# A quantized macaron block with an S4 convolution: byte planes stored by halves, norms with a power on GpSimd, statistics and scales dealt anew

## The chip, the cores and the metric

The kernel runs on one core of a Trainium2 chip. The metric is device time in microseconds (us) of one execution, lower is better; a time that is given for a kernel is the median of several executions. PE is TensorE (PEld its weight loads), DVE is VectorE, ACT is ScalarE, POOL is GpSimd, SP is SyncE, which computes nothing here and issues most of the DMAs.

## What is computed

The input `u` has 2 x 1024 rows of 1024 values, so 2048 tokens. Three residual steps follow each other:

```python
x = x + 0.5 * ffn(layernorm(x))   # 4-bit weights, three matrices
x = x + s4(layernorm(x))          # long convolution over the 1024 values of a row, plus D * row
x = x + 0.5 * ffn(layernorm(x))   # the same weights again

def ffn(x):      # hidden size 1024, inner size 2752
    h = silu(x @ Wg) * (x @ Wu)
    return h @ Wd
# W[k, n] = scales[k // 128, n] * (w4[k, n] - (z4[k // 128, n] + 1))
```

A 32-bit word of a weight matrix holds eight 4-bit numbers, of eight successive rows of one column. Zero points are packed alike, along columns. The layer norm is `(x - mean) / sqrt(var + 1e-5)`.

## The kernel before

The 2048 tokens are four blocks of 512. A *job* is one feed-forward step of one block; eight jobs run in a fixed order (`JOBS`, L782). A job has a gate/up part of 64 *steps* and a down part of 44. In gate/up, the inner size is cut into eight *waves* (0 to 4 with three pairs of column tiles, 5 to 7 with two), and each wave runs over the eight groups of 128 hidden rows, one group a step. A step of waves 0 to 4 is 12 matmuls of 128x128 by 512 (`gate_up`, L826): six column tiles ("units"), each with the high and the low half of the normed input (`xTh`, `xTl`). After each group the sum in PSUM is multiplied by a ratio of scales (`rat`; `scaled`, by ACT at L786 or DVE at L790), so that the weights themselves are plain signed bytes. The down part (L911) works alike with `ratd`.

The bytes are made once, in job 0, and kept in DRAM (`w_q`, `wd_q`), from which every step of every job loads its tile (`load_bytes`, L747 and L754, four steps ahead) and casts it to fp32 (`make_weights`, three steps ahead, by POOL at L763, in job 0 by ACT at L761 for steps that are 1, 2 or 5 modulo 8). Making the bytes of a wave goes like this: `fetch` loads the packed words, `fetch_zeros` loads the table of zero points from DRAM, spread over partitions; `split` (L617 to L632) takes the even and the odd nibbles apart on DVE, adds the zero points and flips signs, in six pieces; `dequantize` (L657) copies each of the eight byte planes (one row out of eight) into a tile `q` on POOL; `keep_bytes` (L667) stores the plane to `w_q` with one DMA from SP. The table of zero points comes from `zero_points_in_pieces` (L381): eight small DVE operations `zi` (L359), one large one `ztab` (L368), and a store to `z_dram` (L388). Wave 0 has its own route (`first_split`, L583), which also puts the bytes of its first group straight into `first_tile`, 16 partitions a plane. The down matrix goes through `fetch_down`, `split_down`, `dequantize_down` (L670 to L698) in six blocks.

What is done when is written by hand. `first_weights` (L700), and `fast` (L1559) for the norms and scales, hang small pieces onto steps: a piece at step 3 is written before that step's matmuls, at 3.5 in their middle. A compiler pass then orders each engine's instructions by its own estimate. Where `in_order_of_writing` (L143) wraps a piece, its instructions keep the written order on the named engines. In job 0 the byte loads keep it on SP for the first 52 steps (L796). Each engine, and SP's queue, works through its instructions in order, so an instruction that waits holds up those behind it.

The work ahead of job 0 is `start` (L1814), pinned in written order on ACT, DVE, SP and PE: loads, `first_split`, the statistics (`first_moments`, two tiles by ACT, two by DVE), the first scales (`scales_in_pieces`, L415), the inverse deviation (`guess` makes a start value by integer arithmetic, `deviations` improves it in three rounds, L219), the normed rows (`first_rows`), and their turn by PE (`first_turn`; ACT copies the high half, DVE subtracts for the low half; chunk 5 goes through POOL). `keep_warm` only keeps PE working.

Of the kernel before, what the change touches and what calls it, by code (L numbers as in the profile page):

```python
# [12 lines left out]
I32 = mybir.dt.int32  # L13
# [44 lines left out]
def macaron_s4_kernel(  # L58
# [43 lines left out]
    qpool = ctx.enter_context(tc.tile_pool(name="q", bufs=4))  # L102
# [79 lines left out]
    def moments_by_tile(b, k, halves=False):  # L182
# [11 lines left out]
        yield from guess_in_pieces(b, k, mv)  # L194

    def guess(b, k, mv):
        for _ in guess_in_pieces(b, k, mv):
            pass

    def guess_in_pieces(b, k, mv):  # L200
        name = f"{b}_{k}"
        ve = small.tile([P, NT], F32, tag="ve", name=f"ve_{name}")
        nc.vector.tensor_scalar(ve, mv[:, :, 1], EPS, None, ALU.add)
        yield
        r = small.tile([P, NT], F32, tag="r", name=f"r_{name}")
        half = small.tile([P, NT], I32, tag="half", name=f"half_{name}")
        nc.vector.tensor_scalar(half, ve.bitcast(I32), 1, None, ALU.logical_shift_right)
        yield
        nc.vector.tensor_scalar(
            r.bitcast(I32), half, -1.0, float(0x5F3759DF), ALU.mult, ALU.add  # L210
        )
        ln[b] = (mv, ve, r)

    def deviations(b, k, factor=1.0):
        for _ in deviations_in_pieces(b, k, factor):
            pass
        return ln[b, 0, "r"]

    def deviations_in_pieces(b, k, factor=1.0, single=False):  # L219
# [3 lines left out]
        for three in (3.0, 12.0, 768.0):  # L223
            nc.vector.tensor_tensor(e, r, r, ALU.mult)
            if single:
                yield
            nc.vector.tensor_tensor(e, e, ve, ALU.mult)
            if single:
                yield
            nc.vector.scalar_tensor_tensor(r, e, three, r, ALU.subtract, ALU.mult)  # L230
            yield
        nc.vector.tensor_scalar(r, r, -factor / 8192, None, ALU.mult)
# [182 lines left out]
    def scales_in_pieces(k0, k1, rows, copy):  # L415
# [14 lines left out]
        copy(flat(s), ps[:, : (u1 - u0) * GK])  # L430
        yield
        inv = t2(f"inv_{k0}")[:, : (u1 - u0) * GK]
        yield from inverse_in_pieces(inv, flat(s), k0)
        yield
        own = rat[:, u0:u1]
        inv = inv.rearrange("p (u g) -> p u g", g=GK)
        nc.vector.tensor_tensor(own[:, :, : GK - 1], s[:, :, : GK - 1], inv[:, :, 1:], ALU.mult)
        nc.vector.tensor_scalar(
# [144 lines left out]
    def first_split(zq):  # L583
# [8 lines left out]
        for part in (even, raw):  # L592
            both = part.bitcast(U16)
            nc.vector.tensor_tensor(both, both, z.bitcast(U16), ALU.add)
        nc.vector.tensor_scalar(both, both, 0x8080, None, ALU.bitwise_xor)

        def rest():
            upper = even.bitcast(U16).rearrange("p (n k) -> p n k", k=2)[:, :, 1]
            nc.vector.tensor_scalar(upper, upper, 0x8080, None, ALU.bitwise_xor)

        def dequantize(j):
            q = t2(f"q_0_{j}").bitcast(I8)[:, :n]
            view = lambda a, dt: a.bitcast(dt).rearrange("p (n k) -> p k n", k=4)[:, j // 2, :]
            if j in (0, 2):
                nc.scalar.activation(q, view(even, U8), AF.Identity, bias=minus_128)
            else:
                nc.gpsimd.tensor_copy(q, view(raw if j % 2 else even, I8))
            nc.sync.dma_start(first_tile[j:P:8], q[: P // 8])
            bytes_of[j] = q

        def keep(j, queue):
            queue.dma_start(w_q[0].rearrange("(r j) n -> j r n", j=8)[j], bytes_of.pop(j))

        bytes_of = {}
        return rest, dequantize, keep
# [40 lines left out]

    def dequantize(w, j):  # L657

        q = qpool.tile([P, width_of(w)], I8, tag="q", name=f"q_{w}_{j}")
        nc.gpsimd.tensor_copy(q, packed[w][j % 2][:, j // 2, :])  # L660
        ready[w, j] = q
        if j == 7:
            packed.pop(w)

    ready = {}

    def keep_bytes(w, j):  # L667
# [1287 lines left out]
```

## Time and profile before

| what | us |
|---|---|
| median of 3 runs | 2049.24 (2048.68 to 2050.22) |
| the profiled execution, its own time | 2049.47 |
| span of its profile | 2047.6 |
| PE, DVE, ACT, POOL busy | 2005.8, 1644.0, 1414.3, 1352.4 |
| first gate/up matmul starts | 21.30 |
| wave 0 / waves 1 to 7 of job 0 end | 56.6 / 201.7 |
| job 0 ends | 291.2 |

The profile is one execution. A row of a stage table has busy times in that stretch. A row of a group has its place in the code, the engine, output and inputs, the count, then the busy time in us and the mean of one in ns, and the idle time before it. A row of the chain shows what the end of the program hung on, followed back; a DMA there is named by what it writes and reads. Names are those of the program with numbers left out: `zi` and `ztab` are the unpacked zero points and their table, `z` the table as read back, `wq` the bytes in DRAM, `b` a tile of bytes, `w_up` the cast weights, `q` a byte plane, `pg` and `po` sums in PSUM.

### The profile page before, as it was taken

The numbers are of one execution on the slowest core, as the hardware profiler recorded it, in microseconds if no ns is written. First come the engines' busy times: TensorE is split into PE (matmuls) and PEld (weight loads), VectorE is DVE, ScalarE is ACT, GpSimd is POOL, SyncE is SP. The second block draws the span as 40 slices with busy tenths as digits, with TensorE's granted clock in tenths as the row PEclk, the third lists the DMA queues.
The fourth block names the chain that finished last, engine by engine and source line by source line (L and its number), as shares of the span: only waits on it lengthen the run. The fifth ranks groups of instructions, "written<-read, shape, count | busy, mean of one in ns | idle before, by whom it ended". The sixth has DMA issues, their size and how long they took to land.

```text
span 2047.6 us, 29913 instructions
## 1 busy us (share of the span) xinstructions
PE 2005.8 (98%) x9198; PEld 1371.3 (67%) x9198; DVE 1644.0 (80%) x2826; ACT 1414.3 (69%) x2217; POOL 1352.4 (66%) x1739
## 2 busy tenths in 40 slices
PE   5999999999999999999999999999999999999998
PEld 3555675567866778665876568667686676866576
DVE  8877978867888787887878777887878978777776
ACT  5788787747676476777777777664776637767775
POOL 4867768757875478755967568763696646965542
PEclk9999999999999999999999999999999999999999
DMA  4335323233624327411462126333163331661113
GB/s 136 114 98 151 114 81 88 56 84 91 174 78 87 88 50 184 150 32 35 117 181 88 32 48 158 97 83 91 38 160 103 72 94 43 155 193 38 34 36 102
DMA packets 347270, 197.14 MB, mean 96 GB/s; under 512 B 168069, under 2 KB 325038, under 8 KB 347102
## 3 DMA queue, kind: packets, MB, share of 16 engines
q1 hardware_dynamic: 345414, 192.55, 35.1%
q10 hardware_dynamic: 1592, 2.41, 0.3%
q8 instruction: 75, 1.23, 0.3%
q14 instruction: 93, 0.76, 0.1%
q0 software_dynamic: 96, 0.20, 0.0%
HBM read 127.52 MB, written 48.57 MB: 86 GB/s over the span
## 4 chain that ended last, share of the span: by engine, by line
PE 92%; DVE 3%; DMA 2%; ACT 1%; issue 1%; POOL 1%; SPq 0%; ACTq 0%; DVEq 0%; POOLq 0%
PE pg L826 57%; PE po L911 30%; PE pc L1279 3%; PE pb L1279 1%; ACT pg L786 1%; DMA b<-wq 1%; DVE pg L790 1%; POOL q L660 0%; DVE hf L861 0%; DMA x<-in_L_attn_u_dram 0%; ACT g L858 0%; POOL w_up L763 0%; DMA z<-z_dram 0%; DVE po L790 0%; PE pt L247 0%
## 5 line engine op out<-in xcount | busy, mean ns | idle before, releaser
L786 ACT ACTIVATE pg<-pg,rat 128x512 f32<-128x512 f32 x1280 | 807.2, 660 | 386.6 <-PE pg L826 382.5
L790 DVE TENSOR_TENSOR pg<-pg,rat 128x512 f32<-128x512 f32 x1128 | 748.5, 692 | 137.3 <-PE pg L826 129.4
L826 PE MATMUL pg<-xTh,w_up 128*128 128x512 f32 x2752 | 848.2, 436 | 3.7 <-ACT pg L786 1.8
L826 PE MATMUL pg<-xTl,w_up 128*128 128x512 f16 x2752 | 710.7, 382 | 10.7 <-ACT pg L786 5.5
L826 PEld LDWEIGHTS pg<-xTh,w_up 128*128 128x128 f32 x2752 | 518.9, 189 | 172.0 <-ACT pg L786 9.0
L763 POOL CAST w_up<-b 128x768 fp32r<-128x768 int8 (+2 forms) x490 | 375.7, 772 | 381.9 <-PE pg L826 261.9
L786 ACT ACTIVATE po<-po,ratd 128x512 f32<-128x512 f32 x669 | 437.8, 662 | 144.5 <-PE po L911 144.0
L911 PE MATMUL po<-hl,w_down 128*128 128x512 f32 x1344 | 526.8, 394 | 1.9 <-DVE po L790 1.8
L911 PE MATMUL po<-hh,w_down 128*128 128x512 f32 x1344 | 521.1, 390 | 0.0
L790 DVE TENSOR_TENSOR po<-po,ratd 128x512 f32<-128x512 f32 x611 | 423.9, 696 | 112.3 <-PE po L911 111.9
L826 PEld LDWEIGHTS <-w_up 128*128 128x128 bf16 x2752 | 227.1, 98 | 346.8 <-issue 163.0
L763 POOL CAST w_down<-bd 128x512 fp32r<-128x512 int8 x352 | 218.6, 624 | 145.1 <-PE po L911 75.7
L911 PEld LDWEIGHTS po<-hl,w_down 128*128 128x128 f32 x1344 | 251.9, 188 | 65.9 <-DVE po L790 6.6
L911 PEld LDWEIGHTS po<-hh,w_down 128*128 128x128 f32 x1344 | 252.4, 188 | 50.5
L865 POOL TENSOR_TENSOR hl<-hf,hh 128x512 fp32r<-128x512 f32 x168 | 218.0, 1298 | 6.6
L863 POOL CAST hh<-hf 128x512 fp32r<-128x512 f32 x168 | 108.7, 647 | 85.7 <-DVE hf L861 58.8
L861 DVE SCALAR_TENSOR_TENSOR hf<-pg,rat,g 128x512 f32<-128x512 f32 x168 | 121.0, 745 | 50.3 <-ACT g L858 43.2
L858 ACT ACTIVATE g<-pg,rat 128x512 f32<-128x512 f32 x168 | 110.1, 688 | 33.5 <-PE pg L826 17.6
L964 POOL TENSOR_TENSOR x<-x,yr 128x512 f32<-128x512 f32 x52 | 66.8, 1285 | 0.0
L299 POOL TENSOR_TENSOR lo<-x,hi 128x512 f16<-128x512 f32 x48 | 62.2, 1297 | 0.0
L189 DVE BATCH_NORM_STATS2 stats<-x 128x6 f32<-128x512 f32 x88 | 59.9, 681 | 0.0
L297 POOL TENSOR_TENSOR mid<-hi,top 128x512 bf16<-128x512 f32 x48 | 56.1, 1168 | 0.0
(215 smaller groups left out, 1075.9 us busy)
## 6 DMA issues: line engine op xcount, KB each, us to landing
b<-wq SPq DMA_DIRECT2D x319, 96.0 KB
bd<-wdq SPq DMA_DIRECT2D x336, 64.0 KB
x<-in_L_attn_u_dram SPq DMA_DIRECT2D x30, 512.0 KB
yz<-y SPq DMA_DIRECT2D x56, 256.0 KB
yr<-yz SPq DMA_DIRECT2D x56, 256.0 KB
b<-wq SPq DMA_DIRECT2D x128, 64.0 KB
sz<-xn SPq DMA_DIRECT2D x16, 512.0 KB
st<-sz SPq DMA_DIRECT2D x64, 128.0 KB
```

What stands on the lines that cost most here:

```text
L299: nc.gpsimd.tensor_tensor(lo[:, own], n[:, own], hi[:, own].bitcast(F32), ALU.subtract)
L763: nc.gpsimd.tensor_copy(t, b)
L786: nc.scalar.activation(dst, src, AF.Copy, scale=sc)
L790: nc.vector.tensor_tensor(dst, src, sc.to_broadcast(list(dst.shape)), ALU.mult)
L826: product = lambda: nc.tensor.matmul(p, weights, (lo, hi)[k][:, g, :], start=(g == 0 and not done), stop=(g == GK - 1 and done), skip_grou ...
L858: nc.scalar.activation(g, pg, AF.Silu, scale=rat[:, 2 * f, GK - 1 :])
L861: nc.vector.scalar_tensor_tensor(hf, pu, last, g, ALU.mult, ALU.mult)
L863: nc.gpsimd.tensor_copy(hi, hf)
L865: nc.gpsimd.tensor_tensor(lo, hf, hi.bitcast(F32), ALU.subtract)
L911: nc.tensor.matmul(ps[c], w[:, bass.ts(c, P)], part, start=(f == 0 and k == 0), stop=(f == NF - 1), skip_group_check=True,)
L964: nc.gpsimd.tensor_tensor(part, part, rows_back.pop((a, t)), ALU.add)
L1279: nc.tensor.matmul(dst, lhsT, rhs, start=start, stop=stop, skip_group_check=True)
```

## The change

The change has six parts.

1. **Stores.** The eight planes of a wave go into one wide tile (from the pool of `y`, which has one buffer), and are stored by two DMAs, one for the four even planes and one for the four odd. In the down matrix, and in wave 0, two planes share a store. The wave's copies and stores get other steps; wave 1's last two split pieces come half a step later.
2. **Load order.** Byte loads keep the written order on SP only in the first 8 steps.
3. **Wave 0 and the start.** All even planes are made by ACT (from unsigned bytes, with a bias of -128), all odd ones by POOL. Wave 1's words are fetched by SP. ACT takes the statistics of one tile, DVE of three. POOL's written order is pinned too. Four of the eight `zi` come ahead of the first turn. Chunk 3 is turned through POOL like chunk 5. In step 0 the high half is multiplied first.
4. **Norms.** `guess` scales the variance and takes its power -0.5 on POOL; `deviations` is one cubic step, of four small DVE operations. The factor `LIFT` moves into `guess`.
5. **Scales.** The copy from PSUM goes to ACT, and the guarded value and the ratios to POOL; DVE keeps the reciprocal.
6. **Down.** Copies come a step later from the third block on, and the third block's split moves to steps 1 to 4.

```diff
-    qpool = ctx.enter_context(tc.tile_pool(name="q", bufs=4))
+    qpool = ctx.enter_context(tc.tile_pool(name="q", bufs=3))
...
-        nc.vector.tensor_scalar(ve, mv[:, :, 1], EPS, None, ALU.add)
...
+        nc.vector.tensor_scalar(ve, mv[:, :, 1], EPS, (8 / (3 * factor)) ** 2, ALU.add, ALU.mult)
         r = small.tile([P, NT], F32, tag="r", name=f"r_{name}")
...
+        nc.gpsimd.tensor_tensor(r, ve, minus_half, ALU.pow)
...
-        for three in (3.0, 12.0, 768.0):
-            nc.vector.tensor_tensor(e, r, r, ALU.mult)
...
+        nc.vector.tensor_tensor(e, r, r, ALU.mult)
+        yield
+        nc.vector.tensor_tensor(e, e, ve, ALU.mult)
+        yield
+        nc.vector.scalar_tensor_tensor(f, e, -10.0 / 3, e, ALU.add, ALU.mult)
+        yield
+        nc.vector.scalar_tensor_tensor(r, f, 5.0, r, ALU.add, ALU.mult)
...
-        copy(flat(s), ps[:, : (u1 - u0) * GK])
...
+        nc.scalar.copy(flat(s), ps[:, : (u1 - u0) * GK])
+        yield
+        safe = t2(f"safe_{k0}")[:, : (u1 - u0) * GK]
+        nc.gpsimd.tensor_tensor(safe, flat(s), flat(s), ALU.mult)
+        nc.gpsimd.tensor_scalar(safe, safe, 2.0**-60, None, ALU.is_lt)
+        nc.gpsimd.tensor_tensor(safe, safe, flat(s), ALU.add)
+        yield
+        nc.vector.reciprocal(safe, safe)
...
+        nc.gpsimd.tensor_tensor(own[:, :, : GK - 1], s[:, :, : GK - 1], safe[:, :, 1:], ALU.mult)
+        nc.gpsimd.tensor_scalar(
...
-        for part in (even, raw):
+        for part in (raw, even):
             both = part.bitcast(U16)
             nc.vector.tensor_tensor(both, both, z.bitcast(U16), ALU.add)
...
-            if j in (0, 2):
+            if j % 2:
+                nc.gpsimd.tensor_copy(q, view(raw, I8))
+            else:
                 nc.scalar.activation(q, view(even, U8), AF.Identity, bias=minus_128)
...
-        q = qpool.tile([P, width_of(w)], I8, tag="q", name=f"q_{w}_{j}")
-        nc.gpsimd.tensor_copy(q, packed[w][j % 2][:, j // 2, :])
...
+        if w not in unpacked:
+            q = ypool.tile([P, 4 * TB], F32, tag="y", name=f"q_{w}").bitcast(I8)[:, : 8 * n]
+            unpacked[w] = q.rearrange("p (two a n) -> p two a n", two=2, a=4)
+        nc.gpsimd.tensor_copy(unpacked[w][:, j % 2, j // 2, :], packed[w][j % 2][:, j // 2, :])
...
+    def keep_bytes(w, odd):
+        rows = w_q[w].rearrange("(r a two) n -> two r a n", a=4, two=2)[odd]
+        nc.sync.dma_start(rows, unpacked[w][:, odd])
...
-            steps = (0.5, 1, 2, 2.5, 2.5, 3) if w == 1 else range(6)
+            steps = (0.5, 1, 2, 2.5, 3, 3.5) if w == 1 else range(6)
...
-            copies = {1: (3,) * 8, 2: (3, 3, 4, 4, 6, 6, 7, 7)}
...
+            copies = {1: (3.5,) * 8, 2: (3, 3, 4, 4, 6, 6, 7, 7)}.get(w, (3, 3, 4, 5, 6, 6, 7, 8))
...
+            for odd, o in enumerate({1: (3.5, 3.5), 2: (5.5, 7.5)}.get(w, (6.5, 9.5))):
+                at(up, s0 + o, lambda w=w, odd=odd: keep_bytes(w, odd))
...
+            return dn, n - 14 if n >= 24 else n - 12 if n > 15 else (0, 0, 1, 2)[n - 12]
...
+                if n == 16:
+                    steps = [(dn, d) for d in (1, 1.5, 2, 2.5, 3, 4)]
...
-            if j == 0 and s < 52:
+            if j == 0 and s < 8:
                 w = in_order_of_writing(next_weights, ET.SP)
...
+            if j == s == 0:
+                turns = [(1 - k, pos, done) for k, pos, done in turns]
...
-        if c != 5:
+        if c not in (3, 5):
...
         dequantize_first, keep_first = first_split(zq)
         for j in (1, 3):
             dequantize_first(j)
+        fetch(1)
         for j in (5, 7):
             dequantize_first(j)
+        first_scales = scales_in_pieces(0, 3, srow)
+        mv, scratch = first_moments()
         next(first_scales)
         for j in (0, 2):
+            dequantize_first(j)
+        next(first_scales)
+        guess(0, 1, mv, LIFT)
+        for _ in first_scales:
+            pass
+        keep_first(1, 0, nc.gpsimd)
+        dequantize_first(4)
+        keep_first(0, 0, nc.sync)
+        dequantize_first(6)
+        keep_first(1, 1, nc.gpsimd)
+        keep_first(0, 1, nc.scalar)
...
         points = zero_points_in_pieces(0, zeros)
-        for _ in range(9):
+        for _ in range(4):
             next(points)
+        first_turn(0)
+        for _ in range(5):
+            next(points)
...
-    points, zeros_down = in_order_of_writing(start, *STARTING, ET.PE)
+    points, zeros_down = in_order_of_writing(start, *STARTING, ET.PE, ET.Pool)
```

## The prediction

> **What bounds the kernel now.** I first cut the span into stages, because an average hides them. Each row gives the stretch, its length, then busy time and instruction count of PE, PEld, DVE, ACT and POOL, then the granted clock and the DMA share.
>
> ```profile
> 0.00:21.30 21.30, 5.11 (x29) 4.60 (x30) 14.51 (x46) 11.16 (x19) 8.07 (x17) 1.00 0.54 186
> 21.30:56.60 35.30, 27.99 (x131) 17.18 (x131) 28.99 (x55) 22.75 (x38) 17.12 (x21) 0.95 0.38 113
> 56.60:104.50 47.90, 45.07 (x200) 26.26 (x199) 41.76 (x66) 37.46 (x61) 41.65 (x44) 1.00 0.38 110
> ...
> 149.60:201.70 52.10, 49.61 (x211) 27.22 (x209) 39.77 (x64) 42.98 (x71) 40.64 (x55) 1.00 0.56 154
> ...
> 291.20:1000.00 708.80, 706.93 (x3281) 480.05 (x3281) 575.06 (x1017) 487.55 (x766) 478.80 (x632) 1.00 0.35 91
> ```
>
> From 291 us on PE idles 1.87 us in 709. There the kernel runs at PE's pace: in job 3, 287 gate/up matmuls take 64.54 us, 0.225 each. What can be won lies in the first 291 us. The first matmul starts at 21.30. Wave 0, the next 35.3 us, holds 8 x 12 = 96 gate/up matmuls, or 21.6 us of work, so 13.7 us are lost (PE's busy time hides half of this: a delayed matmul counts as busy). By the same count waves 1 to 7 (592 matmuls, 133.2 us of work) take 145.1 us from 56.6 to 201.7, so about 12 us are lost, in pieces. Of the last 47.6 us PE is idle 8.5, and the change does not touch the end.
>
> Next I read the chain that ended last, in order of time (start, length, what), for wave 0:
>
> ```profile
> 21.64 2.81 DVE zi L359 x8
> 24.47 1.06 DVE ztab L368
> 25.55 1.82 DMA z_dram<-ztab
> 28.07 4.29 DMA z<-z_dram
> 33.06 4.33 DMA b<-wq
> 37.55 0.92 POOL w_up L763
> 38.47 0.77 POOL q L660
> ...
> 46.62 0.86 POOL q L660
> 47.49 1.62 DMA wq<-q
> 49.75 2.04 DMA b<-wq
> 53.31 3.18 PE pg L826 x7
> ```
>
> This is the making of wave 1's bytes: zero points on DVE, out to DRAM, back spread over partitions, the split, eight byte planes copied by POOL from 38.4 to 47.5, the last plane stored, read back, cast. PE stands still from about 49.9 to 53.3 for it; ACT has the cast of the second of these tiles (L761) at the head of its queue, and the rescales of wave 0 stand behind. Wave 0's end is thus set by this chain, not by the first matmul.
>
> Third, the waits of SP's queue, of POOL and of ACT in the first part (total us, times, longest):
>
> ```profile
> SPq L668 <- POOL q L660: 50.5, 30, 8.8
> ```
> ```profile
> POOL q L660 <- DMA wq<-q: 6.0, 3, 3.3
> ```
> ```profile
> ACT w_up L761 <- DMA b<-wq: 11.0, 5, 3.1
> ```
>
> SP waits 50.5 us in 30 plane stores for POOL's copies, with the byte loads pinned behind them; POOL waits 6.0 us for a free `q` buffer; ACT waits 11.0 us for bytes while rescales stand behind it.
>
> **The change, part by part.**
>
> *The start.* Today DVE has the last statistics at 15.13, because ACT takes two tiles at 2.43 us each, and starts only at 10.22, behind its issue of wave 1's raw words at 9.84. That issue goes to SP, and x's second tile landed at 8.52, so ACT's one tile can be done at 8.55 + 2.43 = 11.0. DVE takes three tiles: split done near 8.8, then 1.28 + 0.21 each, the third having landed at 10.7, so 13.3. The norm loses the shift and magic-number steps: today 3 + 10 small ops at 0.2 us, 15.33 to 17.9; after it 1 + 4 on DVE and one power on POOL. The power has no row. The nearest is POOL's two-input op on few elements:
>
> ```profile
> L1139 POOL TENSOR_TENSOR s_work<-s_work 128x8 f32<-128x8 f32 x28 | 5.1, 204 | 0.6
> L1170 POOL TENSOR_TENSOR s_work<-s_work 128x64 f32<-128x64 f32 x2 | 0.6, 324 | 0.0
> ```
>
> At 0.2 us plus two hand-overs of about 0.1, deviations and bias are ready near 15.1 instead of 18.1. A rule speaks against this: the Trainium skill, GPSIMD Engine Reference, section 2.1 Instruction dispatch, says that the first call of a freshly loaded POOL kernel costs about 6 us without a row of its own. In this trace POOL's first two-input op (L1806, 40.87) took 1.30 us like its later ones (1.29), and its first copy 0.82, so no load shows. By the row the rows start at 15.1; by the rule near 21. I take 0.2 us, as power is an operator of an instruction already in use; no gain is possible below 0.2, and 6 stays as the upper end.
>
> ACT now makes all four even planes (4 x 0.875 from about 11.2, to 14.7) and issues one store, so it is free near 15.2: level with DVE. The last tile piece leaves SP at about 15.4 and lands 1.5 to 2 us later; POOL's cast takes 0.98. The first matmul can start near 18.1, 3.2 earlier.
>
> *DVE between 18 and 26.* Four of the eight zero-point ops (0.36 each) come ahead of the first `xTl`, in time in which DVE would wait for ACT's `xTh` (17.5); that puts `xTl` at 18.0 to 18.7. The four others and the table (1.06) follow, to 21.2, against 25.5 today: 4.3 us earlier, 3 from the start and 1.3 from the scale ops (0.20 + 0.71 + 0.20 + 0.17) that go to POOL. The high half first in step 0 lets PE begin before `xTl` is there, worth 0.6 us, but not on the longer chain, so counted at nothing.
>
> *Wave 1's bytes.* Store and loads of the table follow 4.3 us earlier. The eight copies (6.6 us) and one chunk's turn (2.2 us) remain; chunk 3's turn now falls on POOL too, 2.2 us, at a time in which it waits for bytes (25.2 to 34.4, idle 9.3). If that cover went, 2.2 us would come onto the chain. The odd planes are then stored in one 384-KB piece after the eighth copy. The Trainium skill, DMA: Bandwidth & Descriptors, section Bandwidth, says to batch towards 1 MiB, and with its fixed cost of about 2 us a transfer (section Anatomy of one DMA) six transfers fewer would look like 12 us. The chain shows only the last of eight stores on the path, 1.62 us. The merged one has 24 more packets on each of 16 engines, and a 768-byte packet takes 0.035 us in this trace, so it costs 0.85 more: by the rule a gain, by the row a loss. I take the loss. Sum to wave 1: -4.3 + 0.85 = **-3.4**; bounds -5 (the copies no longer interleaved with the turn) and -1.5 (POOL's scale ops of step 5.5 slip between the copies).
>
> *Waves 2 to 7.* Two stores a wave in place of eight, and byte loads free to go ahead of them after step 8. ACT blocked on bytes is what stops PE in steps 22 and 23 (2.3 us) and 47 (1.5), where the loads at 97.3 and 161.4 left SP right after stores that had waited for late copies. Smaller losses of the kind make 0.6. POOL's wait for `q` buffers within a wave goes as well, but with one wide tile the next wave's first copy waits for both stores: copies of wave 2 end at 70.9 and those of wave 3 start at 71.9, so POOL would stand some 1.5 us there; the casts run about 4 us ahead of PE and hide it. Of 4.4 us I take **-2**; bounds 0 and -4.4. The loads that are freed can also be placed worse; that is a rival below.
>
> *Down, start.* Three pieces of the third block's split leave step 0, where DVE ran splits between rescales and PE showed gaps of 0.88 and 1.20 us at 206.4 and 208.1. Less the usual 0.23 each that is 1.6; **-1**, bounds 0 and -1.6. Copies come a step later; blocks are needed 6 or more steps on, so this costs nothing.
>
> *Norms later on.* Eight small DVE ops fewer in each of 11 norms lie beside PE's work. Only two last ops (L232, 1.23 us where the median is 0.17) held PE, by 0.61 and 0.60 at 884 and 1119: 0.8 in all. That length may belong to the place and not to the op: **-0.4**, bounds -0.8 and +0.4.
>
> *Scales on POOL.* Three groups of about 96 columns, two ops of 0.39, one of about 0.3, then 0.37 and 0.24: 1.7 us each, where POOL is busy 41.65 of 47.9 us. DVE sheds about 1 us each. **+0.6**, bounds -0.5 and +2.
>
> Sum: -3.4 - 2 - 1 - 0.4 + 0.6 = **-6.2**. The profiled execution took 2049.47 us (span 2047.6 and 1.87 around it), 0.23 above the median of 2049.24. So 2043.3 for such an execution, **2043.0** as a median.
>
> **The rivals.**
>
> *All late-byte stalls vanish* (-4.4 in waves 2 to 7, -1.6, -0.8, and -4.4 to wave 1, nothing lost on POOL): -11.2, 2038. For it: SP's 50.5 us behind copies; against it: POOL itself is nearly full from 60 to 80 us, and DVE's slow splits there stay.
>
> *The start gains, wave 1 does not follow.* POOL's scale ops come between its copies (+1.7) and chunk 3's turn loses its cover (+2.2): -6.2 + 3.9 is -2.3, 2047. For it: POOL works without a break from 37.5 to 47.5; against it: it idles 9.3 us just before.
>
> *The power costs 6 us.* The start loses 5.8: 2049.
>
> *Slower: a half-wave store blocks SP.* A store now waits for the fourth copy of its kind, and with load order free a load can stand behind it. Then ACT and PE stop as at 49.8: 3.3 us and 0.5 for twelve matmuls at the lowered clock of 0.83. This would be at the boundaries of waves 2 to 7. From two such blocks on, 7.6 us against a gain of 6.2, the change loses; with the 2 us of waves 2 to 7 lost as well and three blocks it is 2049.2 - 4.2 + 11.4, 2056. Against it: copies of a wave end some 8 us ahead of the next wave's in most waves (wave 3's at 84.1, wave 4's start at 94.5).
>
> **How the numbers follow.** The forecast has a chance of 0.52, all stalls gone 0.20, wave 1 not following 0.14, the costly power 0.04, the blocking store 0.10. A measurement of this kernel can tell about 0.2%, 4.1 us, from no change: faster means below 2045.1, slower above 2053.3. Faster: 0.44 of the forecast's 0.52, the 0.20, and 0.03 of the third, 0.67. Slower: 0.09. Same: 0.24. The forecast's own range is 2039.5 to 2046. The range for 8 in 10 is 2037 to 2048.5: it leaves out the blocking store, half the costly power and the best of the second case, about 0.18.
>
> **What would show it.** In the changed profile: first gate/up matmul near 18; the zero-point table done near 21; PE's stop for wave 1's bytes ending near 50 instead of 53.3; ACT's wait for bytes well under 11 us; the power near 0.2 us; no gaps at the start of down; from 285 us on the same stretches, shifted. The forecast is wrong if the table is early but the POOL copies are not, if new waits of POOL for the wide tile appear, or if SP's loads stand behind half-wave stores.

## The result, and the profile after

The changed kernel takes 2046.55 us (2043.29 to 2047.56, median of 16 runs) where the kernel before took 2049.86 on the same chip (median of 16). The ratio is 0.9981, with a 95% interval from 0.9974 to 0.9989: 0.1 to 0.3% faster. The interval lies below 1, but the gain is less than the 0.2%, or 4.1 us, that the prediction took as the least that can be told. The forecast was 2043.0. The profiled execution of the changed kernel took 2046.72 us, with a span of 2044.9, 2.7 less than before.

The stages of the changed kernel: the start, steps 0 to 8 (wave 0, and the step in which the stop for wave 1's bytes ends), steps 9 to 23 (waves 1 and 2), steps 24 to 62, and a part of the rest. Columns as before: busy time and count of PE, PEld, DVE, ACT, POOL, then the granted clock, the DMA share, GB/s.

```profile
0.00:19.75 19.75, 6.78 (x33) 6.06 (x33) 14.56 (x45) 11.39 (x18) 9.42 (x22) 1.00 0.57 196
19.75:54.07 34.32, 31.29 (x142) 19.18 (x143) 27.81 (x42) 23.98 (x41) 23.62 (x30) 0.95 0.40 119
54.07:101.60 47.53, 43.85 (x188) 25.06 (x187) 38.54 (x59) 35.87 (x59) 40.25 (x47) 0.96 0.37 114
101.60:195.90 94.30, 91.67 (x406) 52.93 (x405) 76.37 (x123) 78.64 (x129) 71.30 (x98) 1.00 0.42 127
287.50:996.20 708.70, 706.32 (x3280) 479.84 (x3280) 569.61 (x976) 486.85 (x766) 482.40 (x637) 1.00 0.34 91
```

Steps 0 to 8 take 34.32 us, and took 37.96 before (21.30 to 59.26); steps 9 to 23 take 47.5, and took 45.20. The second stage gives back a good part of what the first won. The table follows this through every kernel of the study. A step starts with its first gate/up matmul in the trace; the columns are the start of step 9, the stretches from there to step 24 (waves 1 and 2) and to step 63, and the rest of the span. At the right is PE's loss, the time of a step above that of its matmuls at full pace, in the steps that matter.

| kernel | to step 9 | 9 to 24 | 24 to 63 | 63 to end | span | lost in 14, 15 | in 22, 23 | in 47 |
|---|---|---|---|---|---|---|---|---|
| before | 59.26 | 45.20 | 95.16 | 1847.98 | 2047.6 | 0.39 | 2.27 | 1.48 |
| changed | 54.07 | 47.52 | 94.33 | 1848.98 | 2044.9 | 4.76 | 0.0 | 0.0 |
| single planes | 52.91 | 45.04 | 94.54 | 1848.91 | 2041.4 | 2.08 | 0.12 | 0.0 |
| power later | 54.37 | 47.21 | 94.46 | 1846.96 | 2043.0 | 4.45 | 0.14 | 0.0 |
| loads pinned | 54.06 | 47.42 | 94.63 | 1848.79 | 2044.9 | 4.73 | 0.0 | 0.0 |
| tile first | 53.51 | 47.44 | 94.51 | 1849.24 | 2044.7 | 4.39 | 0.15 | 0.0 |
| scales on DVE | 53.79 | 48.05 | 94.29 | 1848.97 | 2045.1 | 5.59 | 0.0 | 0.0 |
| two copies on ACT | 52.23 | 47.32 | 94.44 | 1848.11 | 2042.1 | 4.36 | 0.13 | 0.0 |
| warm PE | 54.69 | 46.72 | 94.51 | 1848.98 | 2044.9 | 3.75 | 0.15 | 0.0 |
| planes, loads pinned | 52.60 | 45.86 | 95.09 | 1848.35 | 2041.9 | 2.50 | 0.14 | 0.55 |
| four buffers | 53.79 | 45.54 | 93.42 | 1850.65 | 2043.4 | 2.25 | 0.21 | 0.60 |
| norms alone | 55.55 | 46.42 | 94.43 | 1848.60 | 2045.0 | 1.61 | 2.31 | 0.74 |
| three edits | 51.68 | 45.30 | 94.46 | 1846.16 | 2037.6 | 2.30 | 0.14 | 0.0 |
| three and tile | 50.78 | 45.24 | 94.43 | 1845.75 | 2036.2 | 2.07 | 0.14 | 0.0 |

So against before: -5.19 to step 9, **+2.32** in waves 1 and 2, -0.83 in waves 3 to 7, **+1.00** afterwards, -2.7 in all.

*The chain of the changed kernel* in order of time, from the last piece of the first tile to wave 2's bytes:

```profile
16.02 2.80 DMA b<-q
...
19.75 2.24 PE pg L842 x6
...
34.06 0.65 POOL xTh L1815
...
37.44 6.37 POOL q L659 x7
...
43.83 2.90 DMA wq<-q
...
47.16 2.17 DMA b<-wq
...
64.85 1.88 POOL q L659 x2
66.75 2.90 DMA wq<-q
...
69.79 1.96 DMA b<-wq
```

From POOL's copies on it is the chain that the prediction described, with wave 1's bytes landing at 49.33 instead of 51.79. Ahead of them it has changed: it now comes from the first tile over PE to the turn of chunk 5 on POOL (34.06), and no longer from the table of zero points; the even bytes, which need the table, are done at 34.25. And it appears twice: wave 2's bytes go the same way, with copies that end at 66.7 and a store of 2.90 us. In both places the load starts only when the whole merged store has landed (43.83 + 2.90 is 46.73, 66.75 + 2.90 is 69.65; the loads leave at once). The single stores took 1.62 in the prediction's chain.

*The waits* that answer to those shown before, of SP's queue, of ACT and of POOL (where the wait stands in brackets), then SP's byte loads behind stores, before and changed:

```profile
SPq L665 <- POOL q L659: 32.4, 8, 10.3
```
```profile
ACT w_up L775 <- DMA b<-wq: 7.2, 3, 3.8
```
```profile
69.79 1.92 POOL L659 COPY q<-even 128x768 int8<-128x768 int8 x2 [2.30 <-DMA wq<-q]
```
```profile
SPq L747 <- DMA wq<-q: 6.8, 7, 1.7
```
```profile
SPq L761 <- DMA wq<-q: 19.4, 9, 3.2
```

SP's waits for copies and ACT's for bytes are fewer than before (30 and 5 times then), but the longest grew, of ACT from 3.1 to 3.8 us. That one is at 68.5 to 72.3, in step 14, for bytes of wave 2. POOL waits once, 2.30 us, for the wide tile of wave 2 to be stored before it can copy wave 3. And byte loads now wait 19.4 us in all for stores to land, where it was 6.8. The last two are signs that the prediction named for being wrong.

*The power.* All calls of it in the changed kernel, with their durations in ns (shortest, median, longest) and who waited:

```profile
L205 POOL TENSOR_TENSOR r<-ve,minus_half x12: 1017/1022/1051, 13.6 to 1694.0; 128x4 f32<-128x4 f32 x12
...
who waited for it (us, times):
  DVE e L218: 2.3, 4
```

It takes 1.02 us on 4 elements a partition, five times the 0.204 of the row that the prediction took, and DVE waits for it four times. One of these places, from the chain:

```profile
707.04 1.03 POOL r L205
...
708.10 0.55 DVE e L218
708.65 0.62 DVE pg L804
...
709.31 1.87 PE pg L842 x7
```

DVE has the norm's next op (L218) at the head of its queue, and behind it a rescale of PSUM that PE needs. From the start of one matmul to the next it is 1.05 us at 708.3, where 0.23 is usual; it is 1.06 at 1435.6 and 0.90 at 1695.4.

*The zero points.* Two views of the kernel before, DVE and POOL, then DVE of the changed one: start, length, engine, line, what and how often.

```profile
21.56 2.88 DVE L359 TENSOR_SCALAR zi<-zq 128x43 int32<-128x43 int32 x8
24.47 1.05 DVE L368 TENSOR_SCALAR ztab<-zi 128x688 uint16<-128x688 int32 x1
```
```profile
21.78 3.37 POOL L763 CAST w_up<-b 128x768 fp32r<-128x768 int8 x4 [1.98 <-DMA b<-wq]
```
```profile
16.89 0.47 DVE L351 TENSOR_SCALAR zi<-zq 128x43 int32<-128x43 int32 x4
...
18.45 0.47 DVE L351 TENSOR_SCALAR zi<-zq 128x43 int32<-128x43 int32 x4
18.95 1.12 DVE L360 TENSOR_SCALAR ztab<-zi 128x688 uint16<-128x688 int32 x1
```

Eight of them took 2.88 us before and take 0.94 now. Before, they lay beside four casts of POOL. The single instructions show how: five took 0.2 each and three 0.87 to 0.89. The first of the three ran from 21.83 to 22.71 while POOL's cast ran from 21.78 to 22.65, and the two others ended at 23.56 and 24.44, against POOL's 23.50 and 24.37. In the changed kernel POOL's next cast starts only at 18.88, when they are done. The Trainium skill, SBUF — State Buffer, section SBUF: two separate sides, describes a port pair that GpSimd and DVE (in a mode of two ports, or with two inputs from SBUF) lock for a whole instruction, the other one blocking; these ends fit it, though no view here shows the mode of an instruction. The run with the norms alone, below, has the same operations without the casts beside them.

*The clock.* PE's stops and what follows: before at wave 1, then changed at wave 1, at wave 2, and behind wave 2.

```profile
49.90:53.30 3.40, 0.26 (x2) 0.10 (x1) 1.65 (x5) 1.43 (x3) 1.94 (x3) 0.96 0.54 143
53.30:56.60 3.30, 3.29 (x9) 1.79 (x9) 0.75 (x2) 2.88 (x5) 1.06 (x3) 0.53 0.64 211
```
```profile
49.80:51.60 1.80, 0.41 (x2) 0.10 (x1) 0.00 (x0) 1.80 (x4) 1.80 (x3) 1.00 0.82 236
70.70:73.70 3.00, 0.45 (x2) 0.01 (x1) 0.33 (x1) 1.39 (x3) 2.84 (x4) 1.00 0.77 215
73.70:78.70 5.00, 4.89 (x13) 2.69 (x14) 2.70 (x4) 4.38 (x9) 4.84 (x9) 0.66 0.83 253
```

The stop for wave 1's bytes is down from 3.4 to 1.8 us, and the clock stays at 1.00 behind it. At wave 2 there is a new stop of 3.0 us, in which PE is busy for 0.45, and for the 5 us behind it the granted clock is 0.66: 13 matmuls in 4.89 us.

### The profile page after: what moved, and what is told of

The parts are those of the page before. It is cut to its first block, busy times and chain, and to the rows that moved or that the text cites. A ratio compares the mean times of both kernels' runs of the same rounds, so it can differ in the third digit from the quotient of the medians.

```text
span 2044.9 us, 29679 instructions
## 1 busy us (share of the span) xinstructions
PE 2008.3 (98%) x9202; PEld 1374.2 (67%) x9202; DVE 1628.9 (80%) x2712; ACT 1413.8 (69%) x2218; POOL 1369.2 (67%) x1772
## 4 chain that ended last, share of the span: by engine, by line
PE 91%; DVE 3%; POOL 2%; issue 1%; DMA 1%; ACT 1%; SPq 0%; DVEq 0%; POOLq 0%; ACTq 0%
PE pg L842 56%; PE po L927 30%; PE pc L1295 3%; PE pb L1295 1%; POOL q L659 1%; DVE pg L804 1%; DMA wq<-q 1%; ACT pg L800 0%; POOL w_up L777 0%; DVE po L804 0%; DVE rawd L623 0%; POOL hl L881 0%; DVE hf L877 0%; DVE rawd L619 0%; DMA b<-wq 0%
```

## The experiments

The theory after the traces: PE comes to step 14 with a lead of 5.2 us (69.40 against 74.65), but wave 2's bytes come only 3.3 us earlier (ACT's first cast of them is at 72.31 against 75.63), and the merged store and the lowered clock make that costly; three norms wait for the power. The main rival: the freed load order makes the stop at steps 14 and 15. "Before" medians in the three groups of runs were 2050.17, 2049.92 and 2049.61. The intervals of all runs but the last two overlap that of the changed kernel (0.9974 to 0.9989), so what a single edit is worth rests on the stages of its trace, one execution each, and not on the total alone.

**Single planes.** The wide tile stays, but waves 1 to 7 are stored in eight DMAs each, at the old times.

```diff
...
-            for odd, o in enumerate({1: (3.5, 3.5), 2: (5.5, 7.5)}.get(w, (6.5, 9.5))):
-                at(up, s0 + o, lambda w=w, odd=odd: keep_bytes(w, odd))
+            stores = {1: (3.5,) * 8, 2: (4.5, 4.5, 5.5, 5.5, 7, 7, 7.5, 7.5)}
+            for k, o in zip(EVEN_FIRST, stores.get(w, [d + 1.5 for d in copies])):
+                at(up, s0 + o, lambda w=w, k=k: keep_plane(w, k))
```

> The changed kernel, but waves 1 to 7 store their planes one by one again (eight stores a wave, out of the same wide tile, at the steps that the kernel before used). Theory A (the wave-2 stop at 70.8 us in the changed kernel, 3.0 us and then a lowered clock, comes from bytes that are about 1 us too late, because the merged odd store takes 2.9 us to land where a single plane took 1.6): wave 2's bytes come 1.0 to 1.3 us earlier, the stop shrinks below 2 us, the clock stays up, step 16 of job 0 starts 2 to 3 us earlier, total -1.5 to -3 us. Rival B (POOL's throughput in waves 0 to 2 is the bound and the store does not matter): step 16 within 0.5 us, total within 1 us. Rival C (merging is what removed the stops at steps 22 and 47): those come back, total +1 to +4 us.

Measured: 2043.21, ratio 0.9965 (0.9952 to 0.9979), 3.3 below the changed kernel. The span is 3.5 shorter: 1.16 by step 9 and 2.48 in waves 1 and 2. Its chain at wave 2, and its clock at the place of the stop:

```profile
67.90 2.05 DMA b<-wq
...
70.03 0.41 ACT w_up L776
```
```profile
70.70:73.70 3.00, 1.96 (x8) 0.89 (x8) 1.22 (x3) 3.00 (x7) 2.84 (x7) 1.00 0.78 231
73.70:78.70 5.00, 5.00 (x23) 2.89 (x22) 2.99 (x6) 4.28 (x8) 5.00 (x8) 1.00 0.78 229
```

The load starts at 67.9 instead of 69.8, PE's stop is no longer whole (8 matmuls in these 3 us, not 2), and the clock stays at 1.00: 23 matmuls in the next 5 us where there were 13. By these two traces a merge that moved the start of a load by 1.9 us cost 2.5 here; the lowered clock is part of it. At wave 1, where the clock holds with either, it cost 1.2. The stops at steps 22, 23 and 47 do not come back (0.12 and 0.0), so merging is not what removed them.

**Power later.** The first three pieces of `deviations` of the third norm come half a step later.

```diff
-                    steps = [(up, done + 0.5 + i / (2 if j == 1 else 1)) for i in range(4)]
+                    gaps = (0.5, 1, 1.5, 2) if j == 1 else (1, 2, 3, 3.5)
+                    steps = [(up, done + d) for d in gaps]
```

> The changed kernel, but the first three of the four improvement pieces of the third norm (jobs 2, 5 and 6) come half a step later, so that DVE does not reach the first of them before POOL's power (1.02 us, behind POOL's casts) is done. Theory: the three new gaps of PE in the changed trace (1.05, 1.06 and 0.90 us at 708, 1436 and 1695) were DVE standing at the head of its queue for the power; they go, total -2 to -2.5 us. Rival (the gaps belong to the boundary of a wave and not to the power): they stay, total within 0.7 us.

Measured: 2044.68, ratio 0.9973 (0.9963 to 0.9984), 1.9 below; the span is 1.9 shorter, 2.0 of it after step 63. The three gaps are gone, and the wait for the power is down to one:

```profile
who waited for it (us, times):
  DVE e L218: 0.8, 1
```

**Loads pinned.** SP's written load order for 52 steps, as before.

```diff
-            if j == 0 and s < 8:
+            if j == 0 and s < 52:
```

> The changed kernel, but byte loads keep the written order on SP for the first 52 steps, as before. Theory A (the stops at steps 22 to 23 and 47 went because a wave has two stores in place of eight, so that few loads stand behind a store): they stay away, total within 1 us. Rival C (they went because loads may pass stores): 2 to 4 us come back at steps 22, 23 and 47.

Measured: 2046.80, ratio 0.9982 (0.9973 to 0.9991): the changed kernel's time. Steps 14 and 15 lose 4.73 as before the edit, and no stop comes back at 22, 23 or 47. The rival falls: with merged stores, load order is worth nothing that shows here.

**Tile first.** In the start, the last piece of the first tile leaves SP ahead of the store of wave 0's even planes.

```diff
         dequantize_first(4)
-        keep_first(0, 0, nc.sync)
         dequantize_first(6)
+        keep_first(0, 0, nc.sync)
```

> The changed kernel, but in the start the last 16-partition piece of the first tile leaves SP ahead of the first store of wave 0's even planes, not behind it. Theory A (the first matmul waits for that piece, which left at 16.0 and landed at 18.8, but the end of wave 0 hangs on the zero-point table and POOL's copies): the first matmul starts 0.6 to 1.5 us earlier than 19.75, wave 1 starts within 0.5 us of where it did, total within 0.7 us. Rival (the start is on the path to the end): total -0.6 to -1.5 us.

Measured: 2045.67, ratio 0.9978 (0.9970 to 0.9986). The first matmul starts 0.75 earlier, at 19.00, step 8 at 49.58 as before the edit (49.60), step 9 0.56 earlier, and the span is 0.2 shorter. The 0.9 between the medians is less than their intervals: by this run alone it can't be told from nothing.

**Scales on DVE.** The later groups' guarded value and ratios back on DVE (`e = nc.vector if k0 else nc.gpsimd` for the five ops).

> The changed kernel, but for the three later groups of scales the guarded value and the ratios are made by DVE again (five small operations a group; the reciprocal stays where it is). Theory (scales on POOL cost about as much there, 1.6 us of POOL at 43.8 to 47.2 and at 74.2 to 75.8, as they save on DVE): the copies of waves 2 and 3 end up to 1.6 us earlier, DVE's rescales get later by about as much, total within 1 us. Rival B (POOL's throughput in waves 0 to 2 is the bound): step 16 starts 1.5 us or more earlier and the total is -1.5 to -3 us.

Measured: 2047.66, ratio 0.9987 (0.9979 to 0.9995). The median is 1.1 above the changed kernel's, but the intervals overlap and the stages of the two traces differ by 0.5 at most: the placement can't be told from none. The +0.6 of the prediction is not seen. Step 16 starts no earlier (80.19 against 79.62) with this work off POOL.

**Two copies on ACT.** Two of the eight copies of wave 1 go to ACT.

```diff
-        nc.gpsimd.tensor_copy(unpacked[w][:, j % 2, j // 2, :], packed[w][j % 2][:, j // 2, :])
+        copy = nc.scalar.copy if w == 1 and j in (0, 2) else nc.gpsimd.tensor_copy
+        copy(unpacked[w][:, j % 2, j // 2, :], packed[w][j % 2][:, j // 2, :])
```

> The changed kernel, but two of the eight byte planes of wave 1 are copied by ACT, which is idle for about a third of that time, in place of POOL. Theory (wave 0's end hangs on the eight copies of POOL, 0.8 us each, and POOL's lead into wave 2 on when it is done with them): wave 1's bytes and the copies of wave 2 come about 1.6 us earlier, both stops shrink, the clock stays up at wave 2, total -2 to -4 us. Rival (ACT's copies stand ahead of rescales and hold PE by as much): PE stops in steps 4 to 6 and the total is within 1 us.

Measured: 2044.01, ratio 0.9971 (0.9960 to 0.9983), 2.5 below. Step 9 starts 1.84 earlier, step 24 by 2.04. POOL's copies are what the end of wave 1's bytes hangs on. Against what was expected, the stop at wave 2 did not shrink: steps 14 and 15 still lose 4.36, and the clock is at 0.66 from 72 to 77. Of the 2.8 in the span 0.9 lies after step 63, where this edit does nothing that I can name.

**Warm PE.** Twelve PE transposes without use, in the middle of step 14, during the stop.

```diff
                 first_weights(up, dn, at)
+                at(up, 14.5, pinned(lambda: keep_warm(12), ET.PE))
```

> The changed kernel with twelve small PE transposes of a constant put in the middle of step 14, where PE stands still for 3.0 us and then works at a clock of 0.66 for 5 us. Theory (1.7 us of the loss there is the clock that falls after the stop): the clock stays at 1.0, step 15 loses 0.4 us in place of 1.7, total -1 to -2 us, while the stop itself keeps its length. Rival (steps 14 and 15 are slow because weights and rescales are late): no gain, or the transposes themselves cost 1 to 2 us.

Measured: 2046.59, ratio 0.9983 (0.9975 to 0.9990). The trace shows the effect in place and not in the total:

```profile
70.70:73.70 3.00, 2.44 (x17) 1.91 (x16) 0.97 (x2) 0.75 (x2) 2.88 (x4) 1.00 0.57 142
73.70:78.70 5.00, 3.84 (x15) 2.02 (x16) 2.27 (x4) 4.89 (x10) 4.84 (x10) 1.00 0.82 246
```

The clock stays at 1.00 and step 15 loses 0.69 instead of 1.68. Steps 9 to 23 take 46.72 instead of 47.52. But this execution started step 9 later, by 0.6, after a slower step 0, and at step 63 both are at 195.92. The gain of 1 to 2 us that was expected of the total did not come. The clock is worth about 1 us at step 15, by this trace alone.

**Planes with pinned loads.** The edits of single planes and of pinned loads together.

> The changed kernel with both single-plane stores (eight a wave) and byte loads in written order for 52 steps, as the kernel before has them, but out of the wide tile. Theory A (the stops at steps 22, 23 and 47 of the kernel before are loads pinned behind many stores): they come back, 2 to 4 us over the run with single planes and free order. Rival D (they came from the four q buffers, for which POOL waited 6 us before): they stay away, the total is that of the run with single planes, within 1 us.

Measured: 2043.78, ratio 0.9968 (0.9956 to 0.9980). The stops at 22 and 23 stay away; 0.55 is back at step 47. So pinned loads alone are not what made the 2.3 us at 22 and 23 of the kernel before; at 47 they may be 0.55 of the 1.48.

**Four buffers.** The same, with `q` tiles from four small buffers again, and the down planes stored singly.

```diff
-    qpool = ctx.enter_context(tc.tile_pool(name="q", bufs=3))
+    qpool = ctx.enter_context(tc.tile_pool(name="q", bufs=4))
...
-        nc.gpsimd.tensor_copy(unpacked[w][:, j % 2, j // 2, :], packed[w][j % 2][:, j // 2, :])
+        unpacked[w, j] = q = qpool.tile([P, width_of(w)], I8, tag="q", name=f"q_{w}_{j}")
+        nc.gpsimd.tensor_copy(q, packed[w][j % 2][:, j // 2, :])
...
```

> Single-plane stores and SP's load order pinned for 52 steps, as in the kernel with planes and pinned loads (2043.8), but the planes of waves 1 to 7 come again from four small buffers in place of one wide tile a wave, as in the kernel before; the down part's planes too come from these buffers and are stored one by one. If the stops of steps 22, 23 and 47 came from POOL waiting for a free small buffer (6.0 us in the kernel before), they return: 2 to 4 us over 2043.8, so 2046 to 2048, and POOL's wait for a store's end is back at about 6 us. If they came from something else in the kernel before (the bunched copies on ACT and DVE, the longer norms), they stay away: within 1 us of 2043.8, with POOL's wait back or not.

Measured: 2044.56, ratio 0.9975 (0.9965 to 0.9985), within 1 us of the wide tile; 22 and 23 lose 0.21. The small buffers alone don't make the stops. The total hides that the trace is 2.0 faster from step 9 to 63 and 2.3 slower after it, where the down planes are now stored singly; no run takes this apart. POOL's last copy of wave 3, in the kernel before and in this one:

```profile
83.29 0.83 POOL L660 COPY q<-raw 128x768 int8<-128x768 int8 x1 [3.25 <-DMA wq<-q]
```
```profile
78.18 0.82 POOL L656 COPY q<-raw 128x768 int8<-128x768 int8 x1 [0.48 <-DMA wq<-q]
```

The wait for a free buffer is 3.25 us before and 0.48 here, with as many buffers. Before, a plane's store also kept its place in SP's written order, behind the words and zero points of the next wave (L718); here only the loads do. The changed kernel frees these stores too, which the list of the change does not say.

**Norms alone.** The kernel before with the new norms and nothing else.

> The kernel before with the new norms alone: the power on POOL and one cubic step in place of the shift, the magic number and three Newton steps. By the prediction's terms: the start gains what DVE's small ops shed, 1 to 2 us of which little reaches the end, and the two long last ops go (0.8): 2048 to 2049. By what the trace of the changed kernel shows: the power takes 1.02 us and three norms wait for it on PE's path (about 2 us lost against 0.8 gained): 2049.5 to 2051.

Measured: 2048.85, ratio 0.9997 (0.9988 to 1.0005): no change that can be told. The trace, of one of the faster of its 13 executions (2047.12), shows what the zero points cost in the kernel before. The first matmul starts at 21.29, as before, but POOL's four casts start 0.8 later (their loads left SP at 20.70, and at 19.84 before), when all eight zero-point operations are done. DVE, then POOL:

```profile
21.54 0.83 DVE L351 TENSOR_SCALAR zi<-zq 128x43 int32<-128x43 int32 x8
22.40 0.52 DVE L360 TENSOR_SCALAR ztab<-zi 128x688 uint16<-128x688 int32 x1
```
```profile
22.59 3.33 POOL L755 CAST w_up<-b 128x768 fp32r<-128x768 int8 x4 [2.03 <-DMA b<-wq]
```

The eight take 0.83 instead of 2.88 and the table 0.52 instead of 1.05, so it is done at 22.92 instead of 25.52. POOL's copies start at 36.23 (38.41 before), and wave 1's bytes land at 49.52 (51.79): with the old start and the old stores that is 2.27 of the 2.46 us by which the changed kernel has them earlier. Step 0 is 1.8 shorter, at a clock of 1.00 in both, since DVE comes to its next `xTl` 1.85 earlier. Step 9 starts at 55.55, 3.7 earlier than before; 1.4 of this is won behind PE's stop, which is as long as before (3.1 us without a matmul) but leaves the clock at 1.00. Steps 14 and 15 take 1.2 of it back, the stops at 22 and 23 are there, 2.31, and behind step 63 it loses 0.6. How often an execution of either kernel meets the casts in this way isn't known; the medians are 0.8 apart.

**Three edits, and four.** Single planes, power later and two copies on ACT; then tile first as well.

> The changed kernel with three of the single edits together: single-plane stores in waves 1 to 7 (-3.3 alone), the third norm's first pieces half a step later (-1.9 alone), two of wave 1's copies on ACT (-2.5 alone). If the places are apart, the first two add and the third adds to them where POOL's copies of wave 1 still end last: 2046.6 - 3.3 - 1.9 - (0 to 2.5), so 2038.9 to 2041.4. If they are the same slack told three times: about 2043.

> The same three edits, and the last piece of the first tile leaves ahead of the store of wave 0's even planes. If the end of wave 1's chain no longer hides the start: 0.7 us below the kernel with three edits. If the start is still off the path: the same within 0.5 us.

Measured: 2039.44, ratio 0.9949 (0.9935 to 0.9962), and 2037.97, ratio 0.9943 (0.9929 to 0.9956). The first is where the sum of the single gains put it: 7.1 of 7.7, the places are apart. With them done, the start does show: step 9 at 50.78 instead of 51.68, 1.4 in the span. These beat both kernels, by 0.5 to 0.6% over before and 0.3 to 0.4% over the changed one; their intervals lie clear of both.

The stretch from step 9 to 24, before, with single planes, and with three edits:

```profile
59.26:104.46 45.20, 42.37 (x188) 24.61 (x187) 39.10 (x64) 35.55 (x58) 38.98 (x41) 1.00 0.37 107
```
```profile
52.91:97.95 45.04, 42.66 (x188) 24.36 (x187) 38.37 (x59) 35.80 (x59) 40.99 (x47) 1.00 0.43 125
```
```profile
51.68:96.98 45.30, 42.46 (x188) 24.44 (x186) 38.55 (x59) 35.67 (x59) 39.44 (x47) 1.00 0.41 120
```

All three take 45 us, with POOL busy 86 to 91% of it. Before, PE lost 0.4 in steps 14 and 15 and 2.3 in 22 and 23; with single planes it loses 2.1 in the first and 0.1 in the second. The loss moved to the place where PE, come early, first meets POOL's bytes; it did not go. The merged stores made it larger. That POOL's throughput is the bound of these waves is likely by this, but not shown: with the scales off POOL, in the kernel with merged stores, they were no shorter.

## Why the prediction was right and wrong

The measured 2046.55 lies in the range for 8 in 10 (2037 to 2048.5) and 0.55 beyond the forecast's own (to 2046); a change too small to be told had a chance of 0.24. That the total is no further off is luck. Against the sum, the traces show 1.8 us more won up to step 9 (5.19 for 3.4), 1.5 lost from there to step 63 where 2 was to be won (less 0.6 for the scales), and 1.0 lost afterwards where 1.4 was to be won.

*To wave 1: the direction was right, the terms were not* (-3.4 foreseen; wave 1's bytes land 2.46 earlier, and step 9 starts 5.19 earlier). The table was done 5.45 us earlier (20.07 against 25.52), not 4.3: the eight `zi` were priced at 0.36 each by a row in which they had stood beside POOL's casts; alone they take 0.2, with starts some 0.09 apart. But the table's store left SP at 21.14, 1.07 behind the table, behind byte loads, so that the first loads of it were issued 4.2 earlier. Not all of this reached POOL: DVE added the zero points only 1.8 earlier (30.91 against 32.67), the even bytes were done 2.7 earlier (34.25 against 36.91), and the copies started 3.7 earlier (34.67 against 38.41), now behind chunk 5's turn. That "store and loads of the table follow 4.3 us earlier" was nearly so; that the copies follow by as much was not, and that 3.7 came so near is in part luck, as another path had taken over. The cover for chunk 3's turn on POOL held. The merged store cost 1.28 (2.90 - 1.62), where 24 packets at 0.035 gave 0.85: the rule on batching, which is one of rate, is no help on this chain, as both row and run say. That leaves 2.46 for the bytes. PE gained more than this for a reason that the sum did not have: it stopped later in its work, in step 8 and not in step 7, for 1.8 us instead of 3.4, and the clock did not fall behind the stop. The clock alone is some 1.5 us, by an estimate from the row at 0.53 (3.3 us times 0.47), and the norms alone show that the old stop could also pass without it.

*The first matmul: -1.55, not -3.2.* Two terms failed. The power took 1.02 us, not 0.2: "POOL's two-input op on few elements", which was taken as the nearest row, was an addition, subtraction or multiplication. But the normed rows were not what the first matmul waited for in the end (both halves were turned by 18.53). The last tile piece stood on SP behind the even planes' store (15.35 to 15.92), left at 16.02 and landed 2.80 later, where "lands 1.5 to 2 us later" was assumed; its cast ended at 19.70. With this piece first, the start came 0.75 earlier, step 8 no earlier and step 9 by 0.56: wave 0's end is not set by the first matmul alone, but in the changed kernel it is no longer free of it. The 6 us for a first call were not seen: the first of the twelve took 1.04, and none over 1.051.

*Waves 2 to 7: this step failed* (-2 foreseen; from step 9 to 63 it is 2.32 - 0.83, so +1.5). The prediction took the losses at steps 22, 23 and 47 for loads behind late stores in SP's queue, and wrote that POOL would stand at the boundary of waves 2 and 3 while "the casts run about 4 us ahead of PE and hide it". The stops did go, but the cause named for them is not shown: pinned loads don't bring those of 22 and 23 back, nor do the small buffers, and the late stores in written order were not tried alone. POOL stood at the boundary for 2.30 us, not 1.5. And the cover of 4 us was that of the old timing, with PE 5 us later. The earlier PE came first to wave 2's bytes, a place that the sum did not look at, and stood there for 3.0 us with the clock at 0.66 behind it: steps 14 and 15 lose 4.76 us where they lost 0.39.

*The slower rival was half right.* "A half-wave store blocks SP" named the stop of 3.3 us, the clock, and a price of 3.8 a block. A stop of 3.0 us with a lowered clock came once, at wave 2, and single planes take 2.5 us of its cost away; that is short of the two blocks from which it decides. But SP's order was not the way: the load waits for the bytes of a store that is late and long.

*Down, start: -1 foreseen, 0 measured.* The gaps of 0.88 and 1.20 became four of 0.50 to 0.77; less the usual 0.23 each their sum is 1.7, and was 1.6.

*Norms later on: -0.4 foreseen.* The two stops at L232 did not go. In the same places the last op of the new norm takes 1.20 and 1.18 us (0.15 in most others), and PE shows 0.55 and 0.54 at 880.9 and 1115.2, after 0.61 and 0.60. DVE and POOL of the changed kernel at the first of them:

```profile
879.59 1.20 DVE L224 SCALAR_TENSOR_TENSOR r<-f,r 128x4 f32<-128x4 f32 x1
```
```profile
879.48 1.29 POOL L881 TENSOR_TENSOR hl<-hf,hh 128x512 fp32r<-128x512 f32 x1
```

DVE's op ends at 880.78, 0.02 behind POOL's; before, L232 ended at 884.42, 0.02 behind the same op of POOL. "That length may belong to the place and not to the op" was right, and it is what the zero points met at the start. The loss is new: three waits for the power cost 2.0 by the run that takes them away. From step 63 on the change stands at +1.0. The price of 0.2 us hid this: a POOL op of 1 us whose result DVE waits for is a wait in front of the rescales.

*Scales on POOL: +0.6 foreseen, nothing to be told apart.*

Open: what made the stops of 22 and 23 before. They are in the two kernels whose plane stores keep SP's written order (before, and norms alone), and in none whose stores are free. That edit alone was not tried, so the prediction's late stores in SP's queue may still be the cause.

## What to carry to other kernels

A lead that is won at one stage is worth only what the next producer can follow: before counting it, compare the time at which PE will come with the time at which the bytes of the next stages come, one by one. Merge transfers where nobody waits for them; on a chain that PE waits for, the last piece sets the time, and a smaller one lands sooner. A stop of PE near 3 us can cost again in the clock. A short DVE operation that runs beside one of POOL can take as long as that one: look at single instructions, not at the mean of a row, before pricing it. An operation in a new form on a known engine should be priced with a wide bound above, and the work behind its consumer in the queue is what its duration costs.

## What the runs showed of the hardware

*The granted clock.* It stayed at 1.00 behind a stop of 1.8 us and fell to 0.66 and 0.53, as means, behind stops of 3.0 and 3.4 us. In the changed kernel the low clock is one stretch of 3.4 us at about half, which starts 1.5 us after PE has begun again. But the length of a stop does not decide it alone: with the norms alone PE stood still for longer (3.08 us without a matmul against 2.60), and the clock stayed. The changed kernel, then norms alone, the stop and what follows:

```profile
75.20:78.60 3.40, 3.39 (x8) 2.01 (x8) 2.26 (x4) 2.78 (x5) 3.32 (x6) 0.51 0.93 280
```
```profile
47.90:51.10 3.20, 0.12 (x3) 0.06 (x2) 1.45 (x5) 1.50 (x3) 1.87 (x3) 1.00 0.62 152
51.10:54.50 3.40, 3.40 (x16) 2.15 (x16) 1.56 (x3) 3.40 (x6) 1.24 (x3) 1.00 0.69 212
```

The Trainium skill, TensorE: Matmul & The Clock Gate, section What's actually happening, has the clock halve after an idle window of about 3.4 us that runs free of the program. The stop of 3.0 us, with 0.45 of work in it, is below that and was enough. A window that runs free would fit that one long stop met it and another did not, and also what the same first step showed in two executions, of the changed kernel and of that with pinned loads, whose code is the same there:

```profile
19.75:25.50 5.75, 5.75 (x24) 4.03 (x25) 2.86 (x6) 2.99 (x6) 3.14 (x4) 0.70 0.41 125
```
```profile
19.58:24.00 4.42, 4.42 (x25) 3.05 (x26) 2.56 (x6) 3.16 (x6) 3.03 (x4) 1.00 0.43 129
```

After nearly the same 5.8 us ahead of it (PE busy for 3.80 and 3.76), step 0 ran at a clock of 0.70 in one and 1.00 in the other, a difference of 1.3 us. Such a difference between single traces is no effect of an edit. Here it did not last either: step 9 starts at 54.07 and 54.06.

*POOL beside DVE.* In the places shown, small DVE operations that started during one of POOL's ended 0.02 to 0.07 us behind it: they took 0.87 to 0.89 us instead of 0.2 (three zero points), and 1.2 instead of 0.15 (the last op of a norm). Zero points that had started ahead of a cast, or at the change from one cast to the next, took 0.2.
